# Dispatching token numbers instead of token rows in a mixture of experts

## The chip, the cores and the metric

The program runs on one core of a Trainium2 chip. A core has five engines that work side by side, each through its own queue, in order: TensorE (PE in the profile; its weight loads are PEld), VectorE (DVE), ScalarE (ACT), GpSimd (POOL) and SyncE (SP). SP computes nothing here; it issues plain data transfers (DMAs). POOL computes a little and issues the indirect DMAs, those whose row numbers are read from a tile. The sixteen DMA engines that move the data are shared by both. The metric is device time in microseconds (us) for the whole program, lower is better.

## The reference, cut to what matters

Two layers act on 3,200 tokens (32 sequences of 100) of 256 numbers each. Each layer is a cross attention to a context, followed by a feed-forward network with experts. Layer 0 has 8 experts, of which each token takes the best 2; layer 1 has 16 experts, of which it takes 4. The change concerns the experts. In layer 0 they are computed like this:

```python
x = x + tanh(g_ffn[0]) * moe(layernorm(x))
# moe(x):
topk_logits, topk_idx = top_k(x_flat @ moe_router, 2)
topk_weights = softmax(topk_logits)
sort_idx = argsort(topk_idx.reshape(tokens * 2))       # token copies in expert order
token_ids_sort = token_ids[sort_idx]
x_sort = x_flat[token_ids_sort]                        # rows of the tokens, gathered
w13_out = ragged_dot(x_sort, moe_w13, group_sizes)
gate, up = split(w13_out, [512], axis=-1)
out_dispatch = ragged_dot(silu(gate) * up, moe_w2, group_sizes)
out_flat = zeros_like(x_flat).at[token_ids_sort].add(out_dispatch * w_sort[:, None])
```

Layer 1 does the same with sigmoid scores, a choice among groups of experts, biases, and a hidden width of 256.

## The kernel before, in words

Four stages follow each other: attention and routing of layer 0 (pool `p0`), experts of layer 0 (`p1`), attention and routing of layer 1 (`p2`), experts of layer 1 (`p3`), and then the output is transposed and stored. A planner in the framework sets the order of the instructions on each engine's queue when the program is built: it plays the program through with expected durations and puts next what it expects to be ready, the earlier written first. Transposes and matrix products of layer 1's attention and routing keep the written order (`mm`, `tr`). On the chip each queue then runs strictly in that order, and every wait between engines is a semaphore.

**Routing and dispatch.** Tokens are handled in 25 tiles of 128, in groups of four (the last group has one). For a group, `residual0` or `residual1` makes the residual of each tile and stores it to `acc` in DRAM (L517, L1094). `route0` or `route1` writes the normalised tile into `row` (L534, L1032), makes the router's scores, and picks the experts. `tile_dispatch` counts how many tokens went to each expert so far, gives every pair of a token and an expert a place in the tensor `sorted` in DRAM (`idx`, L270), adds to each row of `row` its weights for all experts (L271) and its token number (L272), and then scatters the rows of a tile once for each of the 2 or 4 experts chosen (L279), on POOL. Layer 0 has 50 such scatters of 128 rows of 272 numbers, layer 1 has 100 of 288 numbers. The tile `row` holds four token tiles; layer 0 has two such buffers, layer 1 has one.

**Blocks.** When the last tile is dispatched, `blocks` scatters 128 rows of padding behind each expert's tokens (L202: 8 in layer 0, 16 in layer 1), and computes from the counts where each block of 128 rows begins and which expert it belongs to. There are 57 blocks in layer 0 and 115 in layer 1.

**Experts.** The loop at L704 handles the blocks in four steps that overlap: `begin(t)` loads the 128 rows of block t from `sorted` with one plain DMA on SP (L628), transposes them on PE (L631), copies the result (ACT, L633), and takes the block's weight column out of the row (`pick`, DVE, L635, and its sum `w`, L639). `first_product(t)` multiplies with the expert's first weights (L650 or L658), in layer 1 adds the bias (L667), and forms `h` from `silu` (ACT, L669) and the product (DVE, L670). `turn(t)` transposes `h` (L677) and copies it in two halves by DVE (L679) and ACT (L680). `second_product(t)` multiplies with the second weights (L688), copies to `ys` (ACT, L693), and adds the 128 rows to `acc` by an indirect DMA with addition on POOL (L694), whose row numbers are the token numbers at the end of the rows in `x`. In one turn of the loop the order is written as `first_product(t-1)`, `second_product(t-3)`, `turn(t-2)`, `begin(t)`. There are six buffers of `x`, three of `xT`, `h` and `hT`, four of `ys`. All additions go into one tensor, and each waits until the one before has landed.

Of the kernel before, what the change touches and what calls it, by code (L numbers as in the profile page):

```python
# [8 lines left out]
F32 = mybir.dt.float32  # L9
# [8 lines left out]
P = 128  # L18
# [14 lines left out]
T = B * S  # L33
K0, K1 = 2, 4
CAP = T + P
R0, R1 = 272, 288
NT = T // P
AR = 6 * P
PB = DC - P
# [6 lines left out]
def flamingo_kernel(ctx: ExitStack, tc: tile.TileContext, a: dict, out: bass.AP):  # L46
# [74 lines left out]
    class Layer:  # L121
        def __init__(self, nm, n_e, top, f, row, ws):
            self.nm, self.n_e, self.top, self.f, self.row, self.ws = nm, n_e, top, f, row, ws
            self.nt = -(-T * top // P) + n_e - 1
            self.sorted = tc.dram_tile([n_e * CAP + P, row], F32, name=f"sorted{nm}")
            self.acc = tc.dram_tile([T + P, D], F32, name=f"acc{nm}")
            self.pre = const.tile([P, NT + 1, n_e], F32, name=f"pre{nm}")
            nc.vector.memset(self.pre[:, 0, :], 0.0)
            self.pad = padrow[:, :row]
            self.writes = []  # L130
            self.scatter(self.sorted[n_e * CAP :, :], self.pad)

        def free(self, i):

# [1 line left out]
            tc.add_to_no_dep_group(f"sorted{self.nm}", i.ins)  # L136
            return i

        def scatter(self, out, src):
            return self.free(nc.sync.dma_start(out=out, in_=src))  # L140

    nc.vector.tensor_copy(padrow.bitcast(I32)[:, D + E0 : D + E0 + 1], padid)
    la = Layer("a", E0, K0, F0, R0, 1024)
    def load_w13_0(e):
        nc.sync.dma_start(
# [47 lines left out]
    def blocks(wk, L):  # L193


        n_e = L.n_e
        n = L.pre[:, NT, :]
        pad = wk.tile([P, n_e], I32, name=f"pad{L.nm}", bufs=1)
        nc.vector.tensor_tensor(pad, n, padat[:, :n_e], ALU.add)
        for e in range(n_e):  # L200
            L.free(
                nc.gpsimd.indirect_dma_start(  # L202
                    out=L.sorted[:, :],
                    out_offset=bass.IndirectOffsetOnAxis(ap=pad[:, e : e + 1], axis=0),
                    in_=L.pad,
                    in_offset=None,
                )
            )
        full = [P, n_e, NT]
        over_n = wk.tile(full, F32, name=f"over{L.nm}", bufs=1)  # L210
        nc.vector.tensor_tensor(over_n, n.unsqueeze(2).to_broadcast(full), over(steps, full, 1), ALU.is_gt)
        cnt = wk.tile([P, n_e, 1], F32, name=f"blk{L.nm}", bufs=1)
        nc.vector.tensor_reduce(cnt, over_n, AX.X, ALU.add)
        cnt = cnt.rearrange("p e o -> p (e o)")
        ends, s = cnt, 1
        while s < n_e:
            nxt = wk.tile([P, n_e], F32, name=f"ends{L.nm}_{s}", bufs=1)
            nc.vector.tensor_copy(nxt[:, :s], ends[:, :s])
            nc.vector.tensor_tensor(nxt[:, s:], ends[:, s:], ends[:, : n_e - s], ALU.add)
            ends, s = nxt, 2 * s  # L220
# [12 lines left out]
        nc.vector.tensor_scalar(m[:, 1:2], m[:, 1:2], float(n_e * CAP), None, ALU.min)  # L233

        eb = wk.tile([P, P], F32, name=f"eb{L.nm}", bufs=1)
        nc.vector.tensor_scalar(eb, ident, m[:, 2:3], None, ALU.mult)
        ps = bank(f"meta{L.nm}")
        nc.tensor.transpose(ps[:4, :P], m, ident)
        mi = wk.tile([4, P], I32, name=f"mi{L.nm}", bufs=1)
        nc.vector.tensor_copy(mi, ps[:4, :P])  # L240
        ps2 = bank(f"eb{L.nm}")
        nc.tensor.matmul(ps2[:, :P], ones_p, eb, start=True, stop=True)
        ex = wk.tile([P, P], F32, name=f"ex{L.nm}", bufs=1)
        nc.vector.tensor_copy(ex, ps2[:, :P])
        return mi, ex

    def tile_dispatch(wk, L, t0, n, w, member, row, gate, mm=nc.tensor.matmul):
# [19 lines left out]
        for b in range(n):  # L267
# [1 line left out]
        idx = wk.tile([P, NB, 8], I32, tag="ds_i", name=f"idx{L.nm}_{t0}")  # L269
        nc.vector.tensor_scalar(idx[:, :n, :], top[:, :n, :], -1.0, None, ALU.add)  # L270
        nc.vector.tensor_scalar(row[:, :n, D : D + n_e], w, gate, None, ALU.mult)  # L271
        nc.gpsimd.tensor_copy(  # L272
            row.bitcast(I32)[:, :n, D + n_e : D + n_e + 1], idt[:, t0 : t0 + n].unsqueeze(2)
        )
        yield
        for b in range(n):
            for k in range(L.top):
                L.free(
                    nc.gpsimd.indirect_dma_start(  # L279
                        out=L.sorted[:, :],  # L280
                        out_offset=bass.IndirectOffsetOnAxis(ap=idx[:, b, k : k + 1], axis=0),
                        in_=row[:, b, :],
                        in_offset=None,
                    )
                )
# [62 lines left out]
    with tc.tile_pool(name="p0", bufs=2, reuse_waits="tile") as wk, behind(tables):  # L348
# [148 lines left out]
        def residual0(t):  # L497
# [2 lines left out]
            n = min(NB, NT - t0)  # L500
            if t == t0:
                row = wk.tile([P, NB, R0], F32, tag="row", name=f"row0_{t}")
                nc.gpsimd.memset(row[:, :, D + E0 :], 0.0)
                mv = wk.tile([P, NB, 2], F32, tag="mvx", name=f"mvx0_{t}")
                rows[t0] = row, mv, []
            _, mv, xs = rows[t0]
# [85 lines left out]
    def experts(wk, L, mi, ex, w2, bias=None):  # L592
# [31 lines left out]

        def begin(t):
            place(t)
            x = wk.tile([P, L.row], F32, tag="x", name=f"x{L.nm}{t}", bufs=6)
            nc.sync.dma_start(out=x, in_=L.sorted[bass.ds(rows[t], P), :])  # L628
            ps = bank(f"xT{L.nm}{t}")
            for k in range(2):  # L630
                nc.tensor.transpose(ps[:, k * P : (k + 1) * P], x[:, k * P : (k + 1) * P], ident)  # L631
# [5 lines left out]
            )  # L637
            w = wk.tile([P, 1], F32, tag="w", name=f"w{L.nm}{t}", bufs=3)
            nc.vector.tensor_reduce(w, pick, AX.X, ALU.add)  # L639
            st[t] = [x, xT, w]  # L640

        def first_product(t):
            registers(t)
            x, xT, w = st[t]
            o = off[t]
            if f == 512:
                gu = pair(f"gu{L.nm}{t}")
# [33 lines left out]
            st[t].append(hT)  # L681

        def second_product(t):
            x, _, _, _, hT = st.pop(t)
            o = off.pop(t)
            y = bank(f"y{L.nm}{t}")
            for c in range(nf):
# [5 lines left out]
            mark["act"] = nc.scalar.activation(ys, y[:, :D], AF.Copy)  # L693
            nc.gpsimd.indirect_dma_start(  # L694
                out=L.acc[:, :],
                out_offset=bass.IndirectOffsetOnAxis(
                    ap=x.bitcast(I32)[:, D + n_e : D + n_e + 1], axis=0
                ),
                in_=ys[:, :],
                in_offset=None,  # L700
                compute_op=ALU.add,
# [31 lines left out]
        experts(wk, la, mi, ex, w2)  # L733


    nc.vector.memset(padrow[:, D:], 0.0)
    nc.vector.tensor_copy(padrow.bitcast(I32)[:, D + E1 : D + E1 + 1], padid)
    lb = Layer("b", E1, K1, F1, R1, 512)
    for e in range(E1):
        w13 = wres[:, e * 1024 : (e + 1) * 1024].rearrange("p (k f) -> p k f", k=2)  # L740
# [16 lines left out]
    with tc.tile_pool(name="p2", bufs=2, reuse_waits="tile") as wk, behind(tables, mark["pe"]):  # L757
# [235 lines left out]
        def residual1(t):  # L993
# [2 lines left out]
            n = min(NB, NT - t0)  # L996
            if t == t0:
                row = wk.tile([P, NB, R1], F32, tag="row", name=f"row1_{t}", bufs=1)
                nc.gpsimd.memset(row[:, :, D + E1 :], 0.0)
                mv = wk.tile([P, NB, 2], F32, tag="mvx", name=f"mvx1_{t}")  # L1000
                rows[t0] = row, mv, []
            _, mv, xs = rows[t0]
# [234 lines left out]
```

## Time and profile before

| | |
|---|---|
| median of 3 runs | 2804.81 us (2800.51 to 2809.4) |
| the profiled execution | 2807.53 us, its span 2805.8 us |
| PE, PE weight loads | 2250.1 us (80%), 1277.4 us (46%) |
| DVE, ACT, POOL | 1134.3 us (40%), 919.1 us (33%), 481.7 us (17%) |
| data moved | 156.37 MB, 47.75 MB of it by POOL's queue |
| attention and routing, layer 0 | 0 to about 912 us |
| experts, layer 0 | about 912 to 1330 us |
| attention and routing, layer 1 | about 1330 to 2230 us |
| experts, layer 1 | about 2230 to 2767 us |

The profile is one execution, recorded by hardware. Its page lists the busy time of each engine; a table of groups, where a line gives the source line, engine, operation, output and inputs, count, then busy time and mean duration in ns, and after the second bar the time its engine stood idle just before, with what ended that wait; and the chain of work that ended last. The trace can also be read in order of time: each line begins with start and duration in us, and ends in square brackets with the idle time before it and what ended it. A wait for several things is put down to the one that came last by the record; where the engine named had long been done, it was something else. "issue" means that nothing recorded was waited for. SPq and POOLq are the queues of SP and POOL.

### The profile page before, as it was taken

To read this page: it belongs to the slowest core of one execution; us is meant where nothing else is said; L and a number is where in the kernel's file an instruction comes from. 1 tells how busy PE (TensorE), PEld (TensorE's weight loads), DVE (VectorE), ACT (ScalarE), POOL (GpSimd) and SP (SyncE) were. 2 spreads that over 40 slices of the span, in tenths; PEclk is the share of its full clock that TensorE was granted. 3 is DMA by queue.
4 is the path that set the end of the run, shared out by engine and by line. 5 is a ranking of instruction groups with operands and counts; after the bars stand their busy time and mean duration, and the time that the engine had idled before them with its cause. 6 is when DMAs were issued, how large, how long until landed. Compare 5 with 4: busy or idle time off the path is not lost. (4 is left out here: it accounts for less than half of the span.)

```text
span 2805.8 us, 31912 instructions
## 1 busy us (share of the span) xinstructions
PE 2250.1 (80%) x10647; PEld 1277.4 (46%) x10647; DVE 1134.3 (40%) x3430; ACT 919.1 (33%) x2484; POOL 481.7 (17%) x461
## 2 busy tenths in 40 slices
PE   7999999999995888886699687876865277777774
PEld 3555555555553555554355344444533144444442
DVE  3344444343434221121566464655554233333332
ACT  3443434433332222222355253443432022222220
POOL 0001010100102122222100202112021333333331
PEclk9998999999997999999799787887877599999996
DMA  6000010100103222224411202111010533333334
GB/s 221 20 21 31 20 31 21 36 29 23 33 15 104 38 38 39 39 37 122 113 31 26 66 25 67 39 52 56 24 49 33 185 62 61 62 61 61 62 61 113
DMA packets 133953, 156.37 MB, mean 56 GB/s; under 512 B 21648, under 2 KB 125280, under 8 KB 133664
## 3 DMA queue, kind: packets, MB, share of 16 engines
q1 hardware_dynamic: 100672, 106.58, 13.3%
q0 software_dynamic: 33120, 47.75, 9.8%
q8 instruction: 88, 1.44, 0.2%
q14 instruction: 73, 0.60, 0.1%
HBM read 96.39 MB, written 57.88 MB: 55 GB/s over the span
## 5 line engine op out<-in xcount | busy, mean ns | idle before, releaser
L658 PE MATMUL gub<-wres,xTb 128*128 x460 | 239.7, 647 | 24.4 <-ACT xTb L633 23.7
L694 POOL DMA_INDIRECT accb<-ysb,xb x115 | 179.5, 1561 | 365.6 <-ACT hTb L680 151.1
L650 PE MATMUL gua<-wres,xTa 128*128 x456 | 210.0, 604 | 1.0 <-issue 0.6
L688 PE MATMUL yb<-w,hTb 128*128 x460 | 135.9, 405 | 90.0 <-DVE hTb L679 89.9
L279 POOL DMA_INDIRECT sorteda<-row,idxa x50 | 48.4, 968 | 836.4 <-DVE idxa L270 698.6
L453 ACT ACTIVATE e<-s,neg,rs 100x361 f32<-100x361 f32 x256 | 164.1, 649 | 52.0 <-DVE neg L450 29.9
L688 PE MATMUL ya<-w,hTa 128*128 x456 | 123.3, 394 | 51.2 <-DVE hTa L679 51.2
L477 PE MATMUL o<-aT,v 121*64 121x100 f32 x1536 | 133.0, 265 | 35.0 <-DVE aT L471 32.0
L449 DVE TENSOR_REDUCE neg<-s 100x2 f32<-100x722 f32 x128 | 116.0, 906 | 107.8 <-PE s L447 105.8
L688 PEld LDWEIGHTS yb<-w,hTb 128*128 128x128 f32 x460 | 80.5, 194 | 158.1 <-DVE hTb L679 110.7
L694 POOL DMA_INDIRECT acca<-ysa,xa x57 | 88.6, 1554 | 335.4 <-ACT ysa L693 321.2
L477 PEld LDWEIGHTS o<-aT,v 121*64 121x64 f32 x1536 | 88.9, 138 | 115.7 <-DVE aT L471 47.8
L658 PEld LDWEIGHTS gub<-wres,xTb 128*128 128x128 f32 x460 | 84.9, 198 | 111.7 <-issue 62.8
L635 DVE SCALAR_TENSOR_TENSOR pickb<-number,exb,xb 128x16 f32<-128x16 f32 x115 | 27.0, 235 | 263.9 <-DMA xb<-sortedb 263.9
L650 PEld LDWEIGHTS gua<-wres,xTa 128*128 128x128 f32 x456 | 87.8, 194 | 91.6 <-issue 85.4
L472 ACT ACTIVATE aT<-t 121x300 f32<-121x300 f32 x128 | 53.7, 420 | 226.7 <-DVE aT L471 224.8
L959 ACT ACTIVATE e<-e,neg,ms 100x463 f32<-100x463 f32 x128 | 97.5, 762 | 92.9 <-DVE neg L957 92.8
L635 DVE SCALAR_TENSOR_TENSOR picka<-number,exa,xa 128x8 f32<-128x8 f32 x57 | 12.9, 227 | 283.5 <-DMA xa<-sorteda 283.4
L447 PE MATMUL s<-kT,q 64*100 64x361 f32 x512 | 127.4, 491 | 0.0
L279 POOL DMA_INDIRECT sortedb<-row,idxb x100 | 96.7, 967 | 176.2 <-DVE idxb L270 133.6
L436 DVE COPY v<-v 121x512 f32<-121x512 f32 x96 | 63.4, 688 | 156.9 <-PE v L434 156.9
L688 PEld LDWEIGHTS ya<-w,hTa 128*128 128x128 f32 x456 | 82.1, 190 | 97.0 <-DVE hTa L679 64.7
(334 smaller groups left out, 4276.3 us busy)
## 6 DMA issues: line engine op xcount, KB each, us to landing
xb<-sortedb SPq DMA_DIRECT2D x115, 144.0 KB
cb<-in_ctxT SPq DMA_DIRECT2D x128, 90.8 KB
ca<-in_ctxT SPq DMA_DIRECT2D x64, 136.1 KB
wres<-in_L_w SPq DMA_DIRECT2D x8, 1024.0 KB
xa<-sorteda SPq DMA_DIRECT2D x57, 136.0 KB
w<-in_L_w SPq DMA_DIRECT2D x8, 512.0 KB
wres<-in_L_W1T SPq DMA_DIRECT2D x16, 256.0 KB
wres<-in_L_W3T SPq DMA_DIRECT2D x16, 256.0 KB
```

The costliest lines, as they stand in the source:

```text
L279: nc.gpsimd.indirect_dma_start(out=L.sorted[:, :], out_offset=bass.IndirectOffsetOnAxis(ap=idx[:, b, k : k + 1], axis=0), in_=row[:, b, :] ...
L436: nc.vector.tensor_copy(v[:, j, :], ps[i][:CJ, :])
L447: nc.tensor.matmul(s[:S, i, :SC], q[r, p, cols], kT[r, p, :], start=True, stop=True)
L449: nc.vector.tensor_reduce(neg, s[:S, :, :SC], AX.X, ALU.max, negate=True)
L453: nc.scalar.activation(e[:, i, :SC], s[:S, i, :SC], AF.Exp, bias=neg[:, i : i + 1], scale=rs[:, b : b + 1], accum_out=den[:, 2 * p + i : 2 ...
L472: nc.scalar.activation(aT[:, 1, :], t[:CJ, 1, : NJ * S], AF.Copy)
L477: nc.tensor.matmul(o[i * DH : (i + 1) * DH, p * S : (p + 1) * S], v[:, j, h * DH : (h + 1) * DH], aT[:, i, j * S : (j + 1) * S], start=(j ...
L650: nc.tensor.matmul(gu[:, m, :], xT[:, k, :], wres[:, bass.ds(o * 2 + (k * 1024 + m * 512), 512)], start=(k == 0), stop=(k == 1),)
L658: nc.tensor.matmul(gu[:, 0, :], xT[:, k, :], wres[:, bass.ds(o * 2 + k * 512, 512)], start=(k == 0), stop=(k == 1),)
L688: mark["pe"] = nc.tensor.matmul(y[:, :D], hT[:, c * P : (c + 1) * P], w2[:, bass.ds(o + c * D, D)], start=(c == 0), stop=(c == nf - 1),)
L694: nc.gpsimd.indirect_dma_start(out=L.acc[:, :], out_offset=bass.IndirectOffsetOnAxis(ap=x.bitcast(I32)[:, D + n_e : D + n_e + 1], axis=0), ...
L959: nc.scalar.activation(e[:, i, :SK1], e[:, i, :SK1], AF.Exp, bias=neg[:, i : i + 1], scale=rp[:, i : i + 1], accum_out=den[:, 2 * p + i : ...
```

## The change

Dispatch no longer scatters rows. Each group's rows, with their weights, are stored once in token order to a new DRAM tensor `x` of the layer, by a plain DMA on SP. `sorted` becomes one integer per place, and the scatters on POOL (same number, same places) write only the token number, from the constant tile `idt`; the pads write numbers from `padid`. A block first loads its 128 numbers into `ix` (SP, 16 buffers), and then POOL gathers the 128 rows from the tensor `x` into the tile `x` by an indirect DMA. The accumulate takes its row numbers from `ix`. Rows shrink to 264 and 272 numbers, and the memsets of the padding columns and the copy of the token number into `row` go.

```diff
-R0, R1 = 272, 288
+R0, R1 = D + E0, D + E1
 class Layer:
-            self.sorted = tc.dram_tile([n_e * CAP + P, row], F32, name=f"sorted{nm}")
+            self.sorted = tc.dram_tile([n_e * CAP + P, 1], I32, name=f"sorted{nm}")
+            self.x = tc.dram_tile([T + P, row], F32, name=f"tokens{nm}")
...
-            self.pad = padrow[:, :row]
-            self.writes = []
-            self.scatter(self.sorted[n_e * CAP :, :], self.pad)
+            self.free(nc.sync.dma_start(out=self.sorted[n_e * CAP :, :], in_=padid))
+            nc.sync.dma_start(out=self.x[T:, :], in_=padrow[:, :row])
 def blocks:
                     out_offset=bass.IndirectOffsetOnAxis(ap=pad[:, e : e + 1], axis=0),
-                    in_=L.pad,
+                    in_=padid,
 def tile_dispatch:
         nc.vector.tensor_scalar(row[:, :n, D : D + n_e], w, gate, None, ALU.mult)
-        nc.gpsimd.tensor_copy(
-            row.bitcast(I32)[:, :n, D + n_e : D + n_e + 1], idt[:, t0 : t0 + n].unsqueeze(2)
+        nc.sync.dma_start(
+            out=L.x[t0 * P : (t0 + n) * P, :].rearrange("(b p) r -> p b r", p=P), in_=row[:, :n, :]
         )
...
                         out_offset=bass.IndirectOffsetOnAxis(ap=idx[:, b, k : k + 1], axis=0),
-                        in_=row[:, b, :],
+                        in_=idt[:, t0 + b : t0 + b + 1],
 def residual0, residual1 (each with its own width):
-                nc.gpsimd.memset(row[:, :, D + E0 :], 0.0)
 def begin(t):
             place(t)
+            ix = wk.tile([P, 1], I32, tag="ix", name=f"ix{L.nm}{t}", bufs=16)
+            nc.sync.dma_start(out=ix, in_=L.sorted[bass.ds(rows[t], P), :])
             x = wk.tile([P, L.row], F32, tag="x", name=f"x{L.nm}{t}", bufs=6)
-            nc.sync.dma_start(out=x, in_=L.sorted[bass.ds(rows[t], P), :])
+            nc.gpsimd.indirect_dma_start(
+                out=x[:, :],
+                out_offset=None,
+                in_=L.x[:, :],
+                in_offset=bass.IndirectOffsetOnAxis(ap=ix[:, 0:1], axis=0),
+            )
 def second_product(t):
             nc.gpsimd.indirect_dma_start(
                 out=L.acc[:, :],
-                out_offset=bass.IndirectOffsetOnAxis(
-                    ap=x.bitcast(I32)[:, D + n_e : D + n_e + 1], axis=0
-                ),
+                out_offset=bass.IndirectOffsetOnAxis(ap=ix[:, 0:1], axis=0),
                 in_=ys[:, :],
                 in_offset=None,
                 compute_op=ALU.add,
```

Two writes of token numbers into `padrow` ahead of the layers, and the memset ahead of layer 1's, are removed with it.

More of the change, by code (lines that the diff above doesn't have):

```diff
@@ L137, in free @@
             return i
-        def scatter(self, out, src):
-            return self.free(nc.sync.dma_start(out=out, in_=src))
-    nc.vector.tensor_copy(padrow.bitcast(I32)[:, D + E0 : D + E0 + 1], padid)
     la = Layer("a", E0, K0, F0, R0, 1024)
@@ L639, in begin @@
             nc.vector.tensor_reduce(w, pick, AX.X, ALU.add)
-            st[t] = [x, xT, w]
+            st[t] = [ix, xT, w]
         def first_product(t):
             registers(t)
-            x, xT, w = st[t]
+            _, xT, w = st[t]
             o = off[t]
@@ L683, in second_product @@
         def second_product(t):
-            x, _, _, _, hT = st.pop(t)
+            ix, _, _, _, hT = st.pop(t)
             o = off.pop(t)
@@ L733, in flamingo_kernel @@
         experts(wk, la, mi, ex, w2)
-    nc.vector.memset(padrow[:, D:], 0.0)
-    nc.vector.tensor_copy(padrow.bitcast(I32)[:, D + E1 : D + E1 + 1], padid)
     lb = Layer("b", E1, K1, F1, R1, 512)
@@ L998, in residual1 @@
                 row = wk.tile([P, NB, R1], F32, tag="row", name=f"row1_{t}", bufs=1)
-                nc.gpsimd.memset(row[:, :, D + E1 :], 0.0)
                 mv = wk.tile([P, NB, 2], F32, tag="mvx", name=f"mvx1_{t}")
```

## The prediction

> **What bounds the kernel now.** The program runs four stages one after another, so I first cut the span by stage. The view by stretches gives the two expert stages, the only places where the new gather runs (columns: stretch and its length, then busy us and count for PE, PE weight loads, DVE, ACT, POOL, then the granted clock, DMA share and GB/s):
>
> ```profile
> 912.00:1330.00 418.00, 354.44 (x1256) 211.09 (x1255) 82.21 (x231) 99.53 (x230) 87.05 (x56) 0.98 0.28 50
> 2230.00:2767.00 537.00, 409.04 (x1380) 223.98 (x1378) 200.46 (x574) 143.30 (x461) 178.52 (x115) 0.95 0.38 59
> ```
>
> No engine is full in either, so each stage has a loop of waits. Layer 0 has 57 blocks in 418 us. Its loop is seen in the waits of SP's queue and on DVE in order of time:
>
> ```profile
> SPq L628 <- DMA accb<-ysb,xb: 436.7, 109, 16.1
> SPq L628 <- DMA acca<-ysa,xa: 342.6, 51, 20.4
> ```
> ```profile
> 1100.14 0.75 DVE L670 SCALAR_TENSOR_TENSOR ha<-gua,wa,sa 128x512 f32<-128x512 f32 x1 [0.31 <-ACT sa L669]
> 1100.93 0.16 DVE L639 TENSOR_REDUCE wa<-picka 128x1 f32<-128x8 f32 x1
> 1101.18 0.42 DVE L679 COPY hTa<-hTa 128x256 f32<-128x256 f32 x1
> 1107.53 0.23 DVE L635 SCALAR_TENSOR_TENSOR picka<-number,exa,xa 128x8 f32<-128x8 f32 x1 [5.92 <-DMA xa<-sorteda]
> 1107.67 0.75 DVE L670 SCALAR_TENSOR_TENSOR ha<-gua,wa,sa 128x512 f32<-128x512 f32 x1
> ```
>
> The load of block t (L628) waits for the accumulate of block t-6, because that accumulate reads its row numbers out of the old `x` buffer, and there are six. The load therefore lands late, and DVE, which works in order, stands at the `pick` of a block that nobody needs yet. Behind it stands `ha`, whose input `sa` was ready at 1106.49 (ACT started it at 1105.89, 0.60 us): it starts 1.18 us late. In the block before, `ha` did not wait for `pick`. PE then waits for `hT`:
>
> ```profile
> L688 PE MATMUL ya<-w,hTa 128*128 x456 | 123.3, 394 | 51.2 <-DVE hTa L679 51.2
> ```
>
> Undelayed blocks show 0.30 us of this wait, delayed ones 1.26. The starts of the first product are 6.38 us apart in undelayed blocks and 7.1 on average.
>
> Layer 1 has the same late load, but another loop is longer. POOL in order of time, and then the last accumulate from the chain that ended last:
>
> ```profile
> 2499.91 1.55 POOL L694 DMA_INDIRECT accb<-ysb,xb  x1 [3.06 <-ACT hTb L680]
> 2504.32 1.55 POOL L694 DMA_INDIRECT accb<-ysb,xb  x1 [2.85 <-ACT hTb L680]
> 2508.87 1.55 POOL L694 DMA_INDIRECT accb<-ysb,xb  x1 [3.00 <-ACT ysb L693]
> ```
> ```profile
> 2766.39 3.77 DMA accb<-ysb,xb
> ```
>
> Accumulates follow each other every 4.53 us: 3.77 until one has landed and 0.76 until the next starts. The ACT results named as releasers had long been done; it is the landing. They add into the same tensor, so they go one by one: 114 x 4.593 (mean) is the 523.6 us between first and last.
>
> The end of layer 1's routing is the third place:
>
> ```profile
> 2177.16 0.96 POOL L279 DMA_INDIRECT sortedb<-row,idxb  x1 [0.30 <-issue]
> 2180.00 0.41 DVE L1032 TENSOR_SCALAR row<-xt,mvx,rsx 128x256 f32<-128x256 f32 x1 [16.41 <-DMA sortedb<-row,idxb]
> 2221.93 0.96 POOL L202 DMA_INDIRECT sortedb<-padrow,padb  x1 [0.31 <-issue]
> 2227.51 19.69 SPq L628 DMA_DIRECT2D xb<-sortedb  x7
> 2229.67 1.29 PE L631 MATMUL xTb<-ident,xb 128*128 128x128 f32 x4 [29.33 <-DMA xb<-sortedb]
> ```
>
> There is one `row` buffer in layer 1, and 16 scatters of 1.26 us each (2158.13 to 2178.1) read it. The last tile may not overwrite it until they have landed, so its whole routing stands for 16.41 us with nothing beside it.
>
> **The change, part by part.** (a) *`x` is freed by `pick` and the transposes, not by the accumulate* (`ix`, 16 buffers, keeps the numbers). The load can then run some five blocks ahead and `pick` doesn't stop DVE. Layer 0: 54 intervals of the first product (the first two are start-up) sum to 383.5 us; at 6.38 they are 344.5, so 39.0 to gain; by the PE row, 51.2 - 57 x 0.30 = 34.1. I take -36. Layer 1: the accumulates still go one by one, so only the few long gaps can go: (4.593 - 4.53) x 114 = 7 at most. I take -3.
>
> (b) *A gather on POOL for each block.* No gather is in the trace. The nearest row is the scatter of 128 rows of about the same bytes, 0.96 us of POOL and 0.30 to the next; the dearer one is the accumulate, 1.55. In layer 1 the gap between accumulates is 2.98 us; 1.26 fits, and up to about 2.2 us of POOL time would. In layer 0 POOL does 1.55 in 7 us. So 0, if its inputs are ready when its turn comes. If the gaps filled, every us over costs 115 us. From below a gain is excluded, as the landing sets the chain. Behind a gather that waits stands the next accumulate, and behind that the four `ys` buffers, ACT and PE.
>
> (c) *The load of numbers, 172 of them on SP*, 128 x 4 bytes. [...] But SP has nothing else in these stages than such loads and, near the end, weight loads, and with 16 buffers the number is there blocks early; I count the two starts only. There: number load 2.2, then a gather: 0.2 + 0.96 + 1.5 (the last pad scatter of layer 0, 907.11, has landed at 909.60, 2.5 us after its start). That is 4.9 against 2.2, +2.7, and +0.7 because the first product stands behind the transposes of a second block, whose gather comes 1.26 later. +3.4 twice, +6.8.
>
> (d) *Rows go to DRAM once, by SP*, seven times in each layer. `row` is then freed by that store. Its last full one can start at 2155.05; 557 KB at some 370 GB/s is 1.5 us, plus 2.2, done by 2159. The last tile's row then waits only for its own statistics: 2163.59 + 0.90 (as in the group before, 2134.23 to 2135.13) = 2164.5, -15.5 us. The index follows 13.7 us after, 2178.2, when POOL has just ended its 16 scatters; they and the pads move up by the same 15.5. Behind a store on SP stand the next context loads; the `acc` stores have waited there in the same way (316 us in sum at L517) without PE waiting for context, so 0; if that cover fails, the wait is at most some us in each of 14 groups.
>
> (e) *Scatters of 4 bytes.* POOL's time is the same for 1088 and 1152 bytes (0.96), so by descriptor: no gain. [...] Only the last landing before each expert stage is on the path. Against it, 20 scatters and pads of 147 KB leave the stretch 2200 to 2225, where the DMA engines are full (360 to 387 GB/s): 2.9 MB is 8 us of their time, and a 3.2 us stall of the pads and 5.6 us from the last pad to the load (2.5 in layer 0) stand there. Between 0 and -6: -3.
>
> (f) Memsets, copies into `row` and `padrow`: 0.15 to 0.35 us each on a POOL that is idle there. 0.
>
> Sum: -36 - 3 + 6.8 - 15.5 - 3 = -50.7. The profiled execution took 2807.5 (span 2805.8), so 2756.8; the median of the runs is 2804.8, and less 50.7 it is **2754**.
>
> **What it hangs on: POOL's order.** As written, the gather of t comes behind the accumulate of t-3. The order in the queue is the planner's, though, and POOL's trace shows it goes by readiness:
>
> ```profile
> 2097.47 0.73 POOL L1005 TENSOR_TENSOR xt<-xt,bo 128x256 f32<-128x256 f32 x1 [6.96 <-DVE mx L945]
> 2098.14 0.15 POOL L999 MEMSET row<- 128x64 f32 x1
> 2098.35 0.19 POOL L272 COPY row<-idt 128x4 int32<-128x4 int32 x1
> 2098.51 0.73 POOL L1005 TENSOR_TENSOR xt<-xt,bo 128x256 f32<-128x256 f32 x1
> ```
>
> The memset is written ahead of the first of these additions, the copy behind the last; both stand between them. SP too issued layer 1's pad row at 912.67, ahead of 51 loads written before it.
>
> **Rivals.** *Gather behind the accumulate (slower).* If POOL keeps the written order, a loop closes in every block: `ys` ready, 0.28, accumulate 1.55, 0.30, gather 0.96 and 1.5, transposes 0.38, copy 0.38, first product 1.98, second 1.03, `ys` 0.38, waits some 0.8: 9.5 against 4.53 us in layer 1, +570; in layer 0, 12.1 against 7.1, +285. About 3650. It decides when the gather leads by less than about one block. For it: the written order; against it: the four lines above. 8 in 100.
>
> *Gather in the accumulates' gap, but late (slower).* If its `x` buffer comes free only after the landing, the 1.26 joins layer 1's chain: 115 x 1.26 = +145, about 2900; also a gather dearer than 2.2 us of POOL, or PE or SP orders that turn out worse. Against it: PE can run up to four blocks ahead of the accumulates (`ys`). 15 in 100, from 2813 on.
>
> *Layer 0's gain doesn't show*, because another wait takes `pick`'s place: -15, about 2790; 14 in 100, spread from 2785 to 2813. For it: new orders on DVE and PE.
>
> *The forecast*, 63 in 100, own range 2732 to 2785.
>
> **Range and chances.** 2732 to 2845 leaves out the written order and most of the late gathers. The measurement tells 0.3% (8.4 us) from no change; below 2796.4 lie the forecast and 6 of the 14: faster 0.69; same 0.08; slower 0.23.
>
> **What would show it.** Right: no SP wait for an accumulate before the load in the expert stages, DVE's idle time at `pick` gone, layer 0's first products 6.4 us apart; layer 1's accumulates still 4.5; `row` at L1032 not waiting; first transposes 3 us later after the last pad. Wrong: PE waiting for the gathered `x`, accumulates over 4.7 apart, or POOL standing at a gather.

## The result: 0.6% slower, and the profile after

The changed kernel takes 2821.41 us (median of 19 runs, 2803.94 to 2832.83) against 2804.81 us of the kernel before (the median of its 19 runs beside these, too): ratio 1.0057, 95% interval 1.0039 to 1.0075. The forecast was 2754 us, so the sign is wrong. The profiled execution has a span of 2813.6 us, 7.8 us more than before.

I cut both spans at the same events (first products: from the start of the first matrix product to the end of the last):

| stretch | before, us | after, us | difference | forecast |
|---|---|---|---|---|
| layer 0: first scatter of the last full group to the first transposes | 28.5 | 52.8 | +24.3 | +3.4 |
| layer 0: first to last first product of the experts | 397.7 | 364.6 | -33.1 | -36 |
| layer 1: first scatter of the last full group to the first transposes | 71.5 | 82.3 | +10.8 | -15.1 |
| layer 1: first to last accumulate | 523.6 | 530.3 | +6.7 | -3 |
| sum | | | +8.7 | -50.7 |

(-15.1 is -15.5 + 3.4 - 3; of each +3.4 the last 0.7 lies behind the first transposes.) The sum is close to the 7.8 us. What it leaves out nets -0.9 us, from parts that cancel: 3.8 us more ahead of the first stretch, 6.2 us less in layer 1's attention and routing. Layer 0's experts did about what was forecast, layer 1's came out 9.7 us above it. Of the 59.4 us between the two sums, 46.8 lie in the two short stretches ahead of the experts.

The view by stretches of the kernel after, in the columns of the prediction (stretch, its length, busy us of PE, PE weight loads, DVE, ACT, POOL, the granted clock, DMA share, GB/s):

```profile
942.40:1330.00 387.60, 350.02 (x1252) 209.26 (x1252) 84.60 (x227) 97.69 (x229) 143.73 (x119) 0.98 0.30 57
2230.00:2777.00 547.00, 416.46 (x1380) 232.28 (x1380) 199.54 (x575) 142.74 (x461) 300.03 (x228) 0.92 0.36 57
```

POOL has the gathers beside the accumulates, and in layer 0 PE is now busy for 350 of 388 us. The group of the second product, which waited 51.2 us for `hT` before:

```profile
L691 PE MATMUL ya<-w,hTa 128*128 x456 | 122.6, 392 | 21.5 <-DVE hTa L682 21.1
```

SP still waits for accumulates ahead of its loads, but these are the loads of the numbers (L624), with 16 buffers, so they run blocks ahead and nobody stands behind them. The waits of SP's queue (total us, times, longest):

```profile
SPq L624 <- DMA accb<-ysb,ixb: 393.3, 96, 7.8
SPq L624 <- DMA acca<-ysa,ixa: 249.7, 41, 13.7
```

Now the place where the time went. The end of layer 0's routing in order of time (start, duration, then in brackets the idle time before it and what ended it), first POOL, then SP, then PE:

```profile
907.01 0.97 POOL L199 DMA_INDIRECT sorteda<-padid,pada  x1 [0.30 <-issue]
914.67 0.96 POOL L199 DMA_INDIRECT sorteda<-padid,pada  x1 [6.70 <-DMA sorteda<-idt,idxa]
915.94 0.97 POOL L199 DMA_INDIRECT sorteda<-padid,pada  x1 [0.30 <-issue]
936.79 0.98 POOL L626 DMA_INDIRECT xa<-tokensa,ixa  x1 [19.89 <-DMA ixa<-sorteda]
```
```profile
899.23 18.28 SPq L729 DMA_DIRECT2D w<-in_L_w  x5
933.98 5.93 SPq L624 DMA_DIRECT2D ixa<-sorteda  x10
```
```profile
939.90 0.69 PE L634 MATMUL xTa<-ident,xa 128*128 128x128 f32 x2 [35.99 <-DMA xa<-tokensa,ixa]
```

POOL stands 6.70 us between two pads, for an earlier scatter that has not landed. The last pad starts at 915.94, and the first load of the list, which needs every scatter to have landed, leaves at 933.98: 18.0 us later. The kernel before needed 2.5 us there:

```profile
907.11 0.96 POOL L202 DMA_INDIRECT sorteda<-padrow,pada  x1 [0.30 <-issue]
909.60 2.97 SPq L628 DMA_DIRECT2D xa<-sorteda  x6
```

What is under way in the 18 us is the load of the second expert matrix (L729), and it is slow too. The same stretches of 5 us while that matrix is loaded, before and after (same columns; the last two are the DMA share and GB/s):

```profile
895.00:900.00 5.00, 0.80 (x3) 0.53 (x3) 3.38 (x22) 0.00 (x0) 3.36 (x4) 0.50 1.07 384
900.00:905.00 5.00, 0.00 (x0) 0.00 (x0) 0.00 (x0) 0.00 (x0) 3.78 (x5) 0.50 0.94 337
```
```profile
910.00:915.00 5.00, 0.00 (x0) 0.00 (x0) 0.00 (x0) 0.00 (x0) 0.33 (x1) 0.50 0.95 104
915.00:920.00 5.00, 0.00 (x0) 0.00 (x0) 0.00 (x0) 0.00 (x0) 1.60 (x2) 0.50 1.00 113
920.00:925.00 5.00, 0.00 (x0) 0.00 (x0) 0.00 (x0) 0.00 (x0) 0.00 (x0) 0.50 0.79 103
```

The DMA engines are as busy as before and move a third of the bytes. Who occupies them is told by the queues in the stretch 915 to 920 (packets, MB, share of the 16 engines):

```profile
q1 hardware_dynamic: 570, 0.56, 98.8%
q0 software_dynamic: 35, 0.00, 1.0%
```

The scatters (q0) take 1% and the weight load (q1) takes the rest: 0.988 x 16 x 5 us / 570 = 139 ns for a packet of about 1 KB, on average. So the scatters don't fill the engines. By the packets of the trace it is not every packet that slows down: half of the 570 take 46 ns or less, as in the kernel before (895 to 900: 46 ns in the middle, 168 at most). But 37 of them take from 0.5 to 5.5 us, and hold 61% of the time. While these scatters are under way, single packets of the *other* queue are held up.

Layer 1 shows the same. The step that writes the last tile's row no longer waits for the scatters (16.41 us before; now all 25 of its kind together wait 1.5), as forecast. But the pads then stop three times, and the list is loaded 13.7 us after the last of them (5.6 before). Here the scatters' own packets are held up as well: from 2195 to 2200 the 134 of them take 179 ns on average and 30% of the engines' time, though half take 24 ns or less. The group of `row`, then POOL, SP and PE in order of time:

```profile
L1030 DVE TENSOR_SCALAR row<-xt,mvx,rsx 128x256 f32<-128x256 f32 x25 | 8.5, 402 | 1.5 <-ACT rsx L286 0.9 <-DVE mvx L1012 0.6
```
```profile
2188.98 0.96 POOL L199 DMA_INDIRECT sortedb<-padid,padb  x1 [2.43 <-DMA sortedb<-idt,idxb]
2192.78 0.96 POOL L199 DMA_INDIRECT sortedb<-padid,padb  x1 [2.84 <-DMA sortedb<-idt,idxb]
2201.57 0.96 POOL L199 DMA_INDIRECT sortedb<-padid,padb  x1 [7.83 <-DMA sortedb<-padid,padb]
...
2210.46 0.97 POOL L199 DMA_INDIRECT sortedb<-padid,padb  x1 [0.30 <-issue]
```
```profile
2224.19 7.15 SPq L624 DMA_DIRECT2D ixb<-sortedb  x12
```
```profile
2230.11 0.69 PE L634 MATMUL xTb<-ident,xb 128*128 128x128 f32 x2 [49.75 <-DMA xb<-tokensb,ixb]
```

### The profile page after: what moved, and what is told of

It is laid out like the page before. It is cut to its first block, busy times and chain, and to the rows that moved or that the text cites. A ratio compares the mean times of both kernels' runs of the same rounds, so it can differ in the third digit from the quotient of the medians.

```text
span 2813.6 us, 32289 instructions
## 1 busy us (share of the span) xinstructions
PE 2246.5 (80%) x10647; PEld 1280.4 (46%) x10647; DVE 1135.8 (40%) x3427; ACT 917.4 (33%) x2484; POOL 658.7 (23%) x605
## 5 line engine op out<-in xcount | busy, mean ns | idle before, releaser
L276 POOL DMA_INDIRECT sorteda<-idt,idxa x50 | 48.5, 971 | 849.3 <-DVE idxa L267 710.5
L697 POOL DMA_INDIRECT accb<-ysb,ixb x115 | 184.3, 1603 | 208.3 <-DMA accb<-ysb,ixb 52.9
L691 PE MATMUL yb<-w,hTb 128*128 x460 | 141.6, 419 | 89.1 <-DVE hTb L682 83.2
L673 DVE SCALAR_TENSOR_TENSOR ha<-gua,wa,sa 128x512 f32<-128x512 f32 x57 | 42.8, 751 | 274.7 <-ACT sa L672 274.7
L697 POOL DMA_INDIRECT acca<-ysa,ixa x57 | 90.6, 1590 | 221.2 <-DVE picka L638 172.2
L891 POOL TENSOR_SCALAR mb<-mu 100x463 f32<-100x463 uint8 x32 | 18.9, 592 | 502.3 <-DVE mx L944 362.1
L276 POOL DMA_INDIRECT sortedb<-idt,idxb x100 | 97.0, 970 | 167.0 <-DVE idxb L267 132.3
L626 POOL DMA_INDIRECT xb<-tokensb,ixb x115 | 118.0, 1026 | 53.4 <-issue 27.1
```

The costliest lines, as they stand in the source:

```text
L276: nc.gpsimd.indirect_dma_start(out=L.sorted[:, :], out_offset=bass.IndirectOffsetOnAxis(ap=idx[:, b, k : k + 1], axis=0), in_=idt[:, t0 + ...
L626: nc.gpsimd.indirect_dma_start(out=x[:, :], out_offset=None, in_=L.x[:, :], in_offset=bass.IndirectOffsetOnAxis(ap=ix[:, 0:1], axis=0),)
L691: mark["pe"] = nc.tensor.matmul(y[:, :D], hT[:, c * P : (c + 1) * P], w2[:, bass.ds(o + c * D, D)], start=(c == 0), stop=(c == nf - 1),)
L697: nc.gpsimd.indirect_dma_start(out=L.acc[:, :], out_offset=bass.IndirectOffsetOnAxis(ap=ix[:, 0:1], axis=0), in_=ys[:, :], in_offset=None, ...
```

## The experiments

The runs were made in three sets, each set on one chip with its own runs of the kernel before: 2707.35, 2788.28 and 2797.68 us. These differ, mostly in layer 1's attention and routing: from the last first product of layer 0 to the first scatter of layer 1's last full group it takes 753 to 762 us in the first set and 820 to 842 in the others, whatever the kernel. So times are compared as ratios within a set. The experts of layer 0 last 364.4 to 365.8 us (first to last first product) in all sets in every kernel that frees `x` early, so lengths are compared across sets there. The stretch at the end of layer 1's routing is less steady: the same kernel (rows of 64 bytes) has 53.6 us in the first set and 57.5 in the third. The record does not say on which chip the result itself was measured.

My theory after the two traces: 4-byte writes to DRAM land slowly for their size and hold up the other queues. Its rivals: not the size, but that neighbouring numbers share a few bytes of memory, or that the list lies in one small stretch; that scatters and weight loads spoil each other; that the second store of the rows or the gather costs the time.

**The list spread out: the same 4-byte writes, 512 bytes apart.**

```diff
-self.sorted = tc.dram_tile([n_e * CAP + P, 1], I32, ...)
+self.sorted = tc.dram_tile([(n_e * CAP + P) * 128, 1], I32, ...)
+self.far = self.sorted.rearrange("(r c) o -> r (c o)", c=128)
...
-nc.vector.tensor_scalar(idx, top, -1.0, None, ALU.add)
+nc.vector.tensor_scalar(idx, top, -1.0, 128.0, ALU.add, ALU.mult)
...
-nc.sync.dma_start(out=ix, in_=L.sorted[bass.ds(rows[t], P), :])
+nc.sync.dma_start(out=ix, in_=L.far[bass.ds(rows[t], P), 0:1])
```

(The places of the pads are multiplied by 128 in the same way.)

> After, with the sorted list spread: each 4-byte number is written 512 bytes from its neighbours (the indices are multiplied by 128), the block's list is read from the same places. Number and size of the writes stay. Theory SIZE (a 4-byte write lands slowly wherever it lies, and holds up the loads of the expert weights on the same DMA engines): nothing changes, 2815 to 2830 us, 18 us from the last pad to the load of the list in layer 0 and 14 us in layer 1, 1024-byte packets of the weight loads still over 110 ns. Theory NEIGHBOURS (writes to the same stretch of memory wait for each other): about 45 us are won back, 2770 to 2785 us, and the list's load leaves about 2.5 us after the last pad in layer 0.

Measured: 2671.78 us, ratio 0.9867 (0.9846 to 0.9888). The list's load leaves 4.4 us after the last pad in layer 0 and 2.6 us in layer 1. The lines of layer 0:

```profile
909.56 0.97 POOL L202 DMA_INDIRECT sorteda<-padid,pada  x1 [0.30 <-issue]
913.95 1.94 SPq L627 DMA_DIRECT2D ixa<-sorteda  x4
```

Size and number of the writes are those of the changed kernel. My theory of the size is refuted, by the run made to confirm it.

**Rows of 64 bytes.**

```diff
-self.sorted = tc.dram_tile([n_e * CAP + P, 1], I32, ...)
+self.sorted = tc.dram_tile([n_e * CAP + P, 16], I32, ...)
+wid = wk.tile([P, NB, 16], I32, tag="wid", ..., bufs=2)
+nc.gpsimd.tensor_copy(wid[:, :n, :], idt[:, t0 : t0 + n].unsqueeze(2).to_broadcast([P, n, 16]))
...
-        in_=idt[:, t0 + b : t0 + b + 1],
+        in_=wid[:, b, :],
```

> After, with 64-byte rows in the sorted list (the token number 16 times) in place of 4-byte ones; the block reads the first column. Theory SIZE with a step at some size above 64 bytes: as after, 2810 to 2830 us. Theory that the cost is that of 4 bytes alone, or of a write that fills no 64 bytes: about 45 us are won back, 2770 to 2785 us. Theory NEIGHBOURS: in between, since 8 rows instead of 128 share 512 bytes.

Measured: 2673.45 us, ratio 0.9877 (0.9849 to 0.9904); the load leaves 2.9 us after the last pad in layer 0, 2.3 us in layer 1.

**Rows of 512 bytes**, cut out of the row tile.

```diff
+self.pad = padrow.bitcast(I32)[:, D + n_e - 127 : D + n_e + 1]
...
-        in_=idt[:, t0 + b : t0 + b + 1],
+        in_=row.bitcast(I32)[:, b, D + n_e - 127 : D + n_e + 1],
```

> After, with 512-byte rows in the sorted list: the last 128 columns of the row tile, the token number in the last of them (so the row tile has its zeroed columns and its copied number again, as before, and is held until its scatters have landed). Theory SIZE: the drain is gone, the list's load leaves 2.5 to 6 us after the last pad in both layers, weight packets of 1024 bytes are back near 50 ns; about 45 us won, of which the row tile of layer 1's last tile, waiting for 16 scatters again, takes back about 15: 2780 to 2800 us. Theory that it is the second store of the rows, or the gather behind the list, and not the small writes: as after, 2810 to 2835 us.

Measured: 2692.78 us, ratio 0.9953 (0.9938 to 0.9968). The load leaves 4.3 and 3.9 us after the last pad, so this too is free of the late landing, and no better for it than rows of 64 bytes. The wait of layer 1's last tile is back, as expected: 71.0 us from the first scatter to the first transposes, against 53.6 with rows of 64 bytes. These 17.4 us are most of the 19.3 us between the two medians. Store and gather are in all three kernels, so they are not what cost the time.

**The kernel before, with the row freed early in layer 0 and nothing else.**

```diff
+if bias is None:
+    ix = wk.tile([P, 1], I32, tag="ix", ..., bufs=8)
+    nc.vector.tensor_copy(ix, x.bitcast(I32)[:, D + n_e : D + n_e + 1])
-st[t] = [x, xT, w]
+st[t] = [ix, xT, w]
```

(In layer 1, where there is a bias, `ix` remains a view of `x`.)

> The kernel before, with one thing of the change: in layer 0 VectorE copies the token number out of the loaded row into a tile of its own, which the accumulate uses, so that the row's buffer is freed by the transposes and the pick. Rows are scattered and loaded as before. My theory (the row buffers set layer 0's pace, and the change's gain of 33 us there is this alone): 2768 to 2778 us, first products 6.45 us apart instead of 7.10. Rival (the pace of layer 0 is won by the gather, or by loads that SP no longer has queued): no change, 2800 to 2810 us.

Measured: 2679.03 us, ratio 0.9905 (0.9884 to 0.9926). First products 6.459 us apart on average (7.04 in the kernel before, counted in the same way), 365.3 us from first to last; the group of the second product shows PE's wait gone as in the changed kernel:

```profile
L692 PE MATMUL ya<-w,hTa 128*128 x456 | 122.7, 392 | 21.3 <-DVE hTa L683 21.3
```

So the gain of layer 0 is the buffer alone, and needs no gather. The median gain, 28.3 us, is 4 us below the stage's own (397.7 - 365.3 = 32.4).

**The changed kernel itself, on the chip of the next runs.**

> The changed kernel itself once more, on the chip of this set of runs, as the mark for the runs beside it. If the spread lists of the first set won their 50 us from the list and not from the chip that they ran on, this one is again about 1.006 times the kernel before, with 18 us from the last pad to the list's load in layer 0 and weight packets of 1024 bytes at 110 ns and more; if it was the chip, it is near 0.987 as those were.

Measured: 2801.42 us, ratio 1.0049 (1.0034 to 1.0064). In layer 0 the list's load leaves 11.6 us after the last pad, less than the 18 expected, in layer 1 14.5; the weight packets take 103 ns on average (910 to 915), a little less than the 110 expected. The two stretches are shorter here than in the first profile (46.0 us against 52.8, and 79.2 against 82.3), but the loss is the kernel's, not the chip's.

**The 4-byte list in another order, in the same small piece of memory.**

```diff
+nc.vector.tensor_scalar(lo, idx, P - 1, None, ALU.bitwise_and)
+nc.vector.tensor_scalar(hi, idx, 7, None, ALU.logical_shift_right)
+nc.vector.scalar_tensor_tensor(idx, lo, float(L.cols), hi, ALU.mult, ALU.add)
...
-nc.sync.dma_start(out=ix, in_=L.sorted[bass.ds(rows[t], P), :])
+nc.sync.dma_start(out=ix, in_=L.far[:, bass.ds(rows[t], 1)])
```

> After, with the 4-byte list in another order in the same small stretch of memory: place p of the list lies at (p mod 128) x 217 + p / 128 in layer 0 (433 in layer 1), so that the 128 numbers of a block are 868 bytes apart (1732 in layer 1), while the whole list keeps its 111 KB (222 KB); VectorE works out the places, three short operations a group more. Theory NEIGHBOURS (writes in flight at the same time to the same 64 bytes or so wait for each other): as with the spread list, ratio 0.985 to 0.992, list's load 2.5 to 6 us after the last pad. Theory SMALL STRETCH (what counts is that the whole list lies in one small piece of memory, and so behind one port of it): nothing is won, ratio 1.003 to 1.008, 18 us after the last pad.

Measured: 2757.19 us, ratio 0.9896 (0.9845 to 0.9946). POOL, SP and PE in order of time at the end of layer 0's routing:

```profile
915.10 0.97 POOL L209 DMA_INDIRECT sorteda<-padid,pada  x1 [0.31 <-issue]
916.38 0.97 POOL L209 DMA_INDIRECT sorteda<-padid,pada  x1 [0.30 <-issue]
922.07 0.99 POOL L637 DMA_INDIRECT xa<-tokensa,ixa  x1 [4.73 <-DMA ixa<-sorteda]
```
```profile
919.64 5.07 SPq L635 DMA_DIRECT2D ixa<-sorteda  x9
```
```profile
924.93 0.69 PE L645 MATMUL xTa<-ident,xa 128*128 128x128 f32 x2 [11.67 <-DMA xa<-tokensa,ixa]
```

The load leaves 3.3 us after the last pad (2.2 us in layer 1), and no pad stands. And the queues in a stretch of 5 us with the weight load and four pads (910 to 915):

```profile
q1 hardware_dynamic: 1750, 1.74, 107.7%
q0 software_dynamic: 140, 0.00, 2.1%
```

Here a packet of the weight load takes 1.077 x 16 x 5 / 1750 = 49 ns, against 139 above and 103 on this chip, and the longest takes 78 ns. Same bytes, same number of writes, same footprint; apart from the short operations on VectorE only where the neighbours lie differs. The small stretch is excluded too. What counts here is that numbers written at the same time lie side by side: from the last pad to the load 11.6 us in the first order on this chip, 3.3 in this one. On this one chip the two orders are 44.2 us apart by the medians, 15.8 us of it in layer 0's stretch and 22.7 in layer 1's.

**Without the weight loads.**

```diff
-nc.sync.dma_start(out=w2[...], in_=a["L0_w2"][e]...)
+nc.scalar.activation(w2[...], wres[...], AF.Copy)
```

(the same for layer 1's second matrix and its bias)

> After, without the loads of the second expert matrix and of layer 1's bias at the start of both expert stages (ScalarE copies other weights into these tiles, so the output is not the reference's). Theory that the scatters drain slowly by themselves, and the loads only suffer with them: the list's load still comes 12 to 18 us after the last pad in layer 0, the gap of scatters in flight stays. Theory that scatters and loads spoil each other: without loads the list's load leaves within 5 us of the last pad in both layers, and the time is about 2770 to 2785 us on a chip where the kernel before takes 2805 us.

Measured: 2779.47 us, one execution (the kernel before 2788.28). The SP, POOL and stretch views of layer 0:

```profile
924.29 6.01 SPq L624 DMA_DIRECT2D ixa<-sorteda  x11
```
```profile
917.11 0.97 POOL L199 DMA_INDIRECT sorteda<-padid,pada  x1 [0.30 <-issue]
927.09 0.99 POOL L626 DMA_INDIRECT xa<-tokensa,ixa  x1 [9.01 <-DMA ixa<-sorteda]
```
```profile
915.00:920.00 5.00, 0.00 (x0) 0.00 (x0) 0.00 (x0) 0.00 (x0) 2.47 (x3) 0.50 0.01 0
920.00:925.00 5.00, 0.00 (x0) 0.00 (x0) 0.00 (x0) 0.00 (x0) 0.00 (x0) 0.50 0.00 0
```

Neither expectation is met; the truth lies between. The pads no longer stand, but the load still leaves 7.2 us after the last one (7.8 us in layer 1), with the DMA engines idle. With the neighbours apart and the weight loads present it was 3.3 (2.2). The trace's last packet of a scatter ends 1.7 us after the last pad's start, and then 5.4 us (6.1) pass until the load leaves; with the neighbours apart 0.9 (0.4). So the neighbouring writes are late by some 4 us in layer 0 and 5 to 6 us in layer 1 on their own, and the rest of the delay comes only together with the loads.

**Rows of 32 bytes**: the edit of the 64-byte rows with 8 in place of 16.

> After, with 32-byte rows in the sorted list (the token number 8 times); two rows share 64 bytes. One look for the reach of the effect: 64-byte rows put 31.6 us between the first scatter of the last full group and layer 0's first transposes, 4-byte ones 46 to 53 us, and in layer 1 53.6 us against 79 to 82. If two neighbours in 64 bytes are enough to hold each other up: 36 us or more in layer 0 and 60 us or more in layer 1. If it takes many neighbours, or narrower writes: 30 to 34 us and 52 to 57 us.

Measured: 31.9 us from the first scatter to the first transposes in layer 0 and 58.2 us in layer 1 (64 bytes on the same chip: 31.9 and 57.5); 2771.07 us, one execution (the kernel before 2797.68). Rows of 32 bytes side by side are free of it. Widths between 4 and 32 bytes were not run, nor 4-byte numbers whose successors lie less than 512 bytes away without touching.

**The gather replaced by a plain load.**

```diff
-nc.gpsimd.indirect_dma_start(out=x[:, :], out_offset=None, in_=L.x[:, :], in_offset=...)
+nc.sync.dma_start(out=x, in_=L.x[t % NT * P : (t % NT + 1) * P, :])
```

> After, with the gather of a block's token rows replaced by a plain load of one token tile's rows (block t takes tile t modulo 25, so the experts compute on the wrong tokens and the output is not the reference's); the list is still loaded and still used by the accumulate. Theory that the gather beside the accumulate makes layer 1's chain longer: the accumulate takes 1.55 us on POOL again instead of 1.59 (medians), and its period in layer 1 is back from 4.59 to 4.52 to 4.54 us. Theory that it is the list's load or the weight of the traffic: 1.59 us and 4.58 to 4.60 us stay.

Measured: accumulates 1.55 us long (median) and 4.529 us apart in layer 1 (median), against 1.59 and 4.59; 524.0 us from first to last, against 530.5 with gathers on the same chip (rows of 64 bytes). The whole takes 2805.39 us, one execution, with the 4-byte list still in it. POOL in order of time in layer 1, first the changed kernel, then this one:

```profile
2499.32 1.59 POOL L697 DMA_INDIRECT accb<-ysb,ixb  x1 [1.66 <-DMA accb<-ysb,ixb]
2501.21 1.12 POOL L626 DMA_INDIRECT xb<-tokensb,ixb  x1 [0.30 <-issue]
2502.63 0.98 POOL L626 DMA_INDIRECT xb<-tokensb,ixb  x1 [0.30 <-issue]
2503.91 1.62 POOL L697 DMA_INDIRECT accb<-ysb,ixb  x1 [0.30 <-issue]
2508.55 1.59 POOL L697 DMA_INDIRECT accb<-ysb,ixb  x1 [3.02 <-DVE wb L642]
```
```profile
2501.71 1.55 POOL L692 DMA_INDIRECT accb<-ysb,ixb  x1 [2.97 <-ACT hTb L678]
2506.23 1.55 POOL L692 DMA_INDIRECT accb<-ysb,ixb  x1 [2.96 <-ACT hTb L678]
```

The gathers do fit in the gaps between accumulates; what they cost is 0.06 us of each accumulate's period.

**A version that beats both kernels.** It keeps what gained, without the gather: the early freed row of layer 0 (above), and for the last token tile of layer 1 a row buffer of its own.

```diff
-row = wk.tile([P, NB, R1], F32, tag="row", name=f"row1_{t}", bufs=1)
+row = wk.tile([P, n, R1], F32, tag="row" if n == NB else "row_last", name=f"row1_{t}", bufs=1)
...
-wt = wk.tile([E1, NB * P], F32, tag="wt", name=f"wt_{t0}")
+wt = wk.tile([E1, NB * P], F32, tag="wt", name=f"wt_{t0}", bufs=1)
```

> The kernel before with the copied token number of layer 0 (as in the run that frees the row early), and in layer 1 a buffer of its own for the row of the last token tile, so that it does not wait for the 16 scatters of the group before (a work tile of the residual path gives up its second buffer to make room). If my two gains are right and add up: ratio 0.983 to 0.986 (25 to 33 us in layer 0, 15 us in layer 1). If the last tile's wait is paid again further on (the pads, the load of the weights), the ratio stays at 0.990.

Measured: 2748.19 us, ratio 0.9848 (0.9793 to 0.9902). Then once more, beside the rows of 64 bytes:

> The kernel with 64-byte rows in the list, once more, for a narrower interval and beside the next run: ratio 0.986 to 0.990.

> The kernel before with the early freed row and the own buffer for the last tile's row, once more, for a narrower interval: ratio 0.983 to 0.987, and at or a little below the kernel with 64-byte rows, since it has neither the list's load ahead of the first block (3.4 us a layer) nor the gather beside the accumulates (5 to 6 us in layer 1).

Measured: rows of 64 bytes 2776.5 us, ratio 0.9917 (0.9893 to 0.9941); the version without a gather 2762.26 us, ratio 0.9861 (0.9834 to 0.9889). The stretch at the end of layer 1's routing is 58.0 to 58.3 us in its two profiles (71.5 before, 71.6 with the early freed row alone: -13.2 to -13.6), and the group of `row` shows that its last tile waits for no scatter:

```profile
L1036 DVE TENSOR_SCALAR row<-xt,mvx,rsx 128x256 f32<-128x256 f32 x25 | 8.6, 405 | 1.5 <-ACT rsx L289 1.5
```

With the early freed row alone the ratio was 0.9905, so the two gains add up within the intervals. The version without a gather is 14 us ahead of the rows of 64 bytes: on this chip its accumulates of layer 1 take 521.2 us from first to last against 530.5, and its first transposes of layer 0 come 28.5 us after the first scatter against 31.9; together 12.7.

## Why the prediction was wrong

The step that failed is **(e), the scatters of 4 bytes, put at -3**. I bounded it between 0 and -6 by bytes that leave a full stretch, and asked only when the last scatter lands. In the changed kernel it is the dear part: 52.8 us instead of 31.9 in layer 0 and 82.3 instead of 57.5 in layer 1 (against rows of 64 bytes in the third set), 45.7 us in all; on the one chip that ran both the 4-byte list and its other order, 38.5 us. That is most of the 59.4 us between forecast and measurement. Both of my bounds lay on the side of a gain; the trace of before had no scatter of 4 bytes, so no row bounded the loss, and I let 0 stand in its place. Two effects are behind it. Neighbouring 4-byte writes land late by themselves (by 4 us and 5 to 6 us, with the weight loads left out). And with a weight load under way single packets are held up for up to 5.5 us, which brings the mean of the weight packets from 49 ns to 103 and 139, and POOL has to stop at its pads.

The measurement decides that width alone is not what costs: rows of 32 and 64 bytes, and 4-byte writes that lie apart, let the list's load leave 2.2 to 4.4 us after the last pad, and rows of 512 bytes (4.3 and 3.9 us) gained nothing over them. In the run without the weight loads the list's load leaves 5.4 us after the last packet of a scatter (6.1 in layer 1), with the DMA engines idle in layer 0 (a share of 0.01 and 0.00 from 915 to 925). What it waits for in that time, and which part of the memory makes neighbours wait, is not shown by these runs.

The other steps:

- **(a) right in layer 0.** -33.1 us in layer 0 for -36, and -32.4 in the run that has this part alone; the rest is that first products come 6.46 us apart (median), not 6.38. Layer 1's -3 was wrong, and not only because of the gather: with plain loads and the early freed buffer the accumulates take 524.0 us from first to last, against 521.2 on the same chip where layer 1's buffer is held as before. What makes the few long gaps there is open.
- **(b) the mechanism right, the size a little off.** The planner did put the gathers ahead: when an accumulate starts, nine or ten gathers more than accumulates have started, where the written order gives three. They take 0.98 us in layer 0 and 1.03 in layer 1 (means; 0.96 forecast). What I put at 0 is +0.06 us an accumulate, 6.7 us in layer 1, and 6.5 to 10.7 against kernels without a gather on the same chips. I had argued that the landing sets the chain and POOL has room; the run with plain loads shows that the accumulate itself gets longer when gathers stand ahead of it (1.59 us against 1.55).
- **(c) right.** With rows of 64 bytes the stretch in layer 0, to the first transposes, is 3.1 to 3.4 us longer than before (+2.7 forecast), and the first product comes another 0.7 us later (+0.7 forecast). In layer 1 the first transposes come 7.7 to 7.9 us after the last pad, as before (7.7): the added load is paid by scatters that land 3.3 us sooner, which is the part of (e) that did come true. That only the two starts pay held too: with a load of the list in every block the first products of layer 0 take 364.6 us from first to last, against 365.3 in the run with the early freed row, which has no such load. The trace of before has no load of 128 x 4 bytes: the 2.2 us that the forecast takes for it, and for the row's store in (d), are those of an `x` load of 136 KB (issued at 909.60, first transposes at 911.82). In the runs the first gather starts 2.4 to 2.9 us after the list's first load leaves (933.98 to 936.79 in layer 0 of the changed kernel).
- **(d) right.** The last tile doesn't wait, and where the late landing is out of the way the stretch is 14.0 to 17.9 us shorter (rows of 64 bytes; -15.1 forecast with the parts of c and e). The kernel with the last tile's own buffer has 13.2 to 13.6 of it (there is no row store in it). A cost of the stores on SP is not clear of the spread: the first scatter of layer 0's last full group starts at 879 to 893 us in the kernels without stores and at 885 to 897 in those with them.
- **(f)** nothing against it was seen.

With the one fault mended (rows of 64 bytes, third set), the four stretches come to +3.4 - 33.3 - 14.0 + 6.9 = -37.0 us against the profile of before, and the span is 35.1 us below it. The medians of that set are only 21.2 us apart. The 13.9 us between lie in which executions were profiled: that of before, from the result's own set, took 9.9 us more than the median of before in the third set, and that of the rows of 64 bytes 4.1 us less than its own median. No trace of before in the third set is there to say in which stage. In the first set the medians are 33.9 us apart. So even without the fault the forecast of -50.7 us was too large.

The rivals: no gather went behind its accumulate, none came late (accumulates 4.59 us apart; late gathers would have put them near 5.8), and layer 0's gain showed. The measured time lies where I had put late gathers, and so inside the range of 2732 to 2845 us, but by none of the mechanisms that I named: that the range holds is luck.

## What to carry to other kernels

Making a transfer smaller is an edit of its own, with a loss to bound as well as a gain: ask where the written bytes lie side by side and what else is loading at that time. As far as these runs go, a list of 4-byte numbers scattered into neighbouring places is better written in rows of 32 bytes or more, or in an order that puts numbers of one scatter apart. The other order won 44 us on the chip that ran both, the rows of 64 bytes some 40 to 50 us by the ratios. And when a buffer is held by one small column of it, copy the column before building a new data path: one 128 x 1 copy a block gave the whole gain of layer 0.

## What the runs showed of the hardware that was not expected

- While scatters of 128 x 4 bytes to neighbouring places were under way, single packets of another queue were held up: 37 of 570 took 0.5 to 5.5 us, half took 46 ns or less, and the mean of about 1 KB went from 49 ns to 103 and 139. The scatters' own packets took 1% of the DMA engines' time in that window of layer 0 and 30% in one of layer 1. In that window of layer 0 a DMA share of 1.00 went with 113 GB/s; in the kernel before 0.94 and 1.07 went with 337 and 384 GB/s, and with rows of 32 or 64 bytes or the other order 1.08 to 1.11 went with 348 to 367.
- 512 bytes or 868 bytes between the numbers, or rows of 32 or 64 bytes, all cure it alike: 30.2 to 32.4 us in layer 0's stretch, against 46.0 and 52.8.
- With idle DMA engines the list's load still leaves 7.2 us after the last such scatter starts in layer 0, against 2.5 to 4.4 after others. For 5.4 us of it the trace has no packet of a scatter.
- An accumulate of 128 rows takes 1.59 us of POOL instead of 1.55 when gathers run between the accumulates.
